# Weighing the values of two tiles together, with a third place for weights and the key norms one tile earlier

## The chip, the cores and the metric

The kernel runs on one core of a Trainium2 chip. The core has TensorE (PE in the profile), VectorE (DVE), ScalarE (ACT), GpSimd (POOL) and SyncE (SP), which issues the transfers here. Each engine works through its own queue of instructions and waits on semaphores that others raise. The metric is the time of one execution on the device in microseconds.

## The reference, cut to what matters

One perceiver layer for 128 queries of width 512, in fp32: a cross attention over 12544 rows of context, a self attention, and a mixture of experts. The change lies wholly in the cross attention, whose text part covers the 12287 context rows behind the first 257:

```python
q = rms_norm(linear(x, q_w, q_b), norm_q_w).reshape(B, L, NH, HD)
k = rms_norm(linear(ctx_txt, k_w, k_b), norm_k_w).reshape(B, -1, NH, HD)
v = linear(ctx_txt, v_w, v_b).reshape(B, -1, NH, HD)
img_x = attention(q, k_img, v_img)     # the 257 image rows, keys and values of their own
txt_x = attention(q, k, v)             # 16 heads of 32 channels, softmax over the rows
out = (txt_x + img_x).reshape(B, L, DIM)
```

## The kernel before

The text rows are cut into blocks of 512 rows (`blocks[1]` to `blocks[24]`; block 0 is the image part) and each block into four tiles of 128 rows, called j = 0 to 3 below. A tile has a running number t. Keys and values of a block come from seven quarter products each instead of eight (a Strassen scheme): `step(b, k)` computes product k of the keys (`kp`) and of the values (`vp`), and the sums of context quarters that it needs come from `ctx_sums` on POOL (L1058, tile `xs`).

For each tile, `scores` (L1159) multiplies keys by queries: 16 small matmuls on 32 rows of the array each, in tiling form 32*128, into the one PSUM tile `s`, which takes four of eight banks. `weights` (L1246) makes `p` from it: VectorE scales each row by `rinv` (the inverse norm of its key) and subtracts the bound `m_bc` (L1255), ScalarE takes the exponential (L1263). `weigh` (L1266) multiplies the values by `p` and adds to `avp`: 16 matmuls in form 128*32. `into_sums` (L1424, L1433) adds `p` to the running sums of weights `ls` on POOL. There are two places for `p` (pool `two`, tag `p`).

The norms of the keys go through four engines. When the keys of half a block are ready, `squares` (L1116) squares them on ScalarE, `add_squares` (L1123, rows L1127) folds the squares to one row of partitions' sums in two POOL instructions, `key_norms` (L1010, rows L1018 and L1029) sums over partitions with 16 tiny matmuls on PE in form 128*32 and scales on VectorE, and `inv_sqrt` (L815, row L818) raises to the power -1/2 on POOL, which gives `rinv`. Half 0 of a block serves its tiles 0 and 1, half 1 its tiles 2 and 3.

The main loop (L1535 to L1640) goes over the tiles of blocks 2 to 23. While it works on block b it makes the keys and values of block b+1. All instructions are pinned (`pin`), so each engine executes them in the order in which the program writes them. For a block b the order on the engines that matter is:

| tile | PE | POOL |
|---|---|---|
| j=0 | products 1; scores; weigh the tile before; products 2 | tile j=3 of the block before into the sums; `add_squares(b, 1)` |
| j=1 | products 6; scores; weigh; norms of b, half 1 | tile j=0 into the sums; `rinv` of b, half 1 |
| j=2 | products 5, 7 of keys; scores; weigh; products 3 | tile j=1 into the sums; in blocks 17 to 22 one scaling of later weights |
| j=3 | product 7 of values; scores; weigh; norms of b+1, half 0; products 4 | `add_squares(b+1, 0)`; tile j=2 into the sums; `ctx_sums(b+2)`; `rinv` of b+1, half 0 |

In the table `weigh` always means the tile before the one whose scores were just made (`weigh_pending`, L1448, with `pend`). The last block, 24, follows written out (L1642 to L1676), where the loads for the self attention begin (`early_loads`, L1486) as places come free. The place `mb`, which held the first bound, is free after tile 13; in block 15 two loads of weight codes go there (L1633 to L1635). Here t1 is the first text tile, `RENEWED` is 2, `SWITCH` is tile 13, `LAST` is 24, `AHEAD` is blocks 17 to 22.

Of the kernel before, what the change touches and what calls it, by code (L numbers as in the profile page):

```python
# [9 lines left out]
FP = mybir.dt.float32  # L10
# [5 lines left out]
P = 128  # L16
# [754 lines left out]
def fast_block(ctx: ExitStack, tc: tile.TileContext, a: dict, out: bass.AP, amiss: bass.AP):  # L771
# [78 lines left out]
    def load_codes(g, nm, t):  # L850

        codes[g, nm] = t.rearrange("p (c f) -> p c f", c=4)
        pin(nc.sync.dma_start(out=codes[g, nm], in_=a[f"w{nm}_codes"][g]))
# [28 lines left out]
    def slot(pool, tag, name):  # L882

        t = pool.tile([P, 2, 1024], FP, tag=tag, name=name)
        return [t[:, 0, :], t[:, 1, :]]
# [10 lines left out]
    with ExitStack() as xs:  # L896
# [226 lines left out]
        def add_squares(b, i):  # L1123

            ks = slice(i * HALF, (i + 1) * HALF)
            for w in (2, 1):
                pin(nc.gpsimd.tensor_tensor(  # L1127
                    sq[b][:, :w, ks], sq[b][:, :w, ks], sq[b][:, w : 2 * w, ks], op=ALU.add
                ))
# [318 lines left out]
        def weigh_pending():  # L1448
            k, pk = pend
            weigh(k, pk, k in (t1, SWITCH), k == SWITCH - 1)  # L1450
# [35 lines left out]
        def early_loads(j):  # L1486

            if j == 0:
                f = slot(two, "kraw", "f")
                homes[2].append(f[0])  # L1490
                load_codes(2, "v", f[0])
                homes[3] = [f[1]]
                load_codes(3, "q", f[1])
                homes["bv"] = slot(two, "ctx", "bv")
                wo.append(slot(xc, "kw", "wo_0"))
            elif j == 1:
                g = slot(two, "v", "g")
                homes[3] += g
                load_codes(3, "k", g[0])
                load_codes(3, "v", g[1])  # L1500
                t = row("kt", "sc_23", (P, 2, 3 * GW))
                load_scales(2, t[:, 0, :])
                load_scales(3, t[:, 1, :])
                for k, of in enumerate((a["bv"][:1024], a["bv"][1024:])):
                    pin(nc.sync.dma_start(out=homes["bv"][k], in_=of.partition_broadcast(P)))
                wo.append(slot(two, "ctx", "wo_1"))
                wo.append(slot(xc, "xsum", "wo_2"))
                pin(nc.sync.dma_start(
                    out=so, in_=a["wo_scales"].unsqueeze(1).to_broadcast([FEAT // BLOCK, 2, D])
                ))  # L1510
                load_wo(0)
            elif j == 2:
                h = slot(xc, "sq", "h")
                homes[4] = list(h)
                load_codes(4, "q", h[0])
                load_codes(4, "k", h[1])
                t = row("vt", "sc_45", (P, 2, 3 * GW))
                load_scales(4, t[:, 0, :])
                load_scales(5, t[:, 1, :])
                pin(nc.sync.dma_start(out=bo, in_=a["bo"].partition_broadcast(P)))  # L1520
                wo.append(slot(xc, "vw", "wo_3"))
                load_wo(1)
                load_wo(2)
# [3 lines left out]
        def load_wo(k):  # L1527
            for h in range(2):
# [2 lines left out]
                    out=wo[k][h].rearrange("p (j f) -> p j f", j=2), in_=a["wo_codes"][:, j : j + 2, :]  # L1531
                ))

        AHEAD = range(NB - 8, NB - 2)
        for t in range(tile0[2], tile0[LAST]):  # L1535
            b, part, o, m = tiles[t]
            j = t - tile0[b]


            make = step  # L1540
            if t == SWITCH + 3:
                pin(nc.tensor.matmul(
                    avp["txt"].rearrange("p g q -> p (g q)"),
                    lhsT=ident,
                    rhs=kept["av"],
                    start=False,
                    stop=False,
                    skip_group_check=True,
                ))
            late = make if b + 1 < LAST else (lambda *of: None)  # L1550
            if j == 0:
                make(b + 1, 1)
            elif j == 1:
                make(b + 1, 6)
            elif j == 2:
                make(b + 1, 5)
                late(b + 1, 7, "k")
            else:
                late(b + 1, 7, "v")
            if j == 3:  # L1560
                add_squares(b + 1, 0)
            if t == tile0[LAST] - 1:
                unsummed = pend
            else:
                into_sums(*pend)
            if j == 0:
                add_squares(b, 1)
            elif j == 2 and b in AHEAD:
                scale_weights((b - AHEAD[0]) // 3, "qkv"[(b - AHEAD[0]) % 3], nc.gpsimd)
            elif j == 3 and b + 2 < NB:  # L1570
                ctx_sums(b + 2)
            if t == SWITCH:
                m_bc["txt"] = m_new
            p, s = weights(t)
            weigh_pending()
            if j == 1:
                key_norms(b, [2, 3])
            elif j == 3 and b + 1 < LAST:
                key_norms(b + 1, [0, 1])
            pend = (t, p)  # L1580
            if t == tile0[RENEWED + 1]:
                m_new = xc.tile([P, 4, CHUNK], FP, tag="mx", name="mb_new")
                on_all(q_new, m_new, "new")
                pin(nc.vector.tensor_tensor(over, q_new, q_old, ALU.subtract))
                less = small.tile([P, XH], FP, tag="less", name="less")
                pin(nc.scalar.activation(less, over, AF.Exp, scale=-1.0))
            elif t == tile0[RENEWED + 1] + 1:

                shrink = rowp.tile([P, D], FP, tag="h", name="shrink")
                on_heads(less, shrink, "less")  # L1590
            elif t == SWITCH:
                av_old = avp["txt"].rearrange("p g q -> p (g q)")
                kept = {"av": row("kept_av", "kept_av")}
                pin(nc.vector.tensor_tensor(kept["av"], av_old, shrink, ALU.mult))
                avp["txt"] = ps_o.tile([P, NC, P], FP, tag="o", name="av_new")
            elif t == SWITCH + 2:
                lp = bank("l_old")
                for i in range(4):
                    r = slice(i * XHD, (i + 1) * XHD)
                    pin(nc.tensor.matmul(  # L1600
                        lp[r, :], lhsT=ones[:, :XHD], rhs=ls_old[i // 2][:, i % 2, :],
                        start=True, stop=True, skip_group_check=True,
                    ))
                kept["l"] = row("kept_l", "kept_l")
                pin(nc.vector.tensor_tensor(kept["l"], lp, shrink, ALU.mult))
            if j == 2:
                make(b + 1, 3, "k")
            if b <= RENEWED:
                largest(t, s)
            if j == 0:  # L1610
                make(b + 1, 2)
            elif j == 2:
                make(b + 1, 3, "v")
            elif j == 3:
                late(b + 1, 4)
                if b + 3 < NB:
                    load_ctx(b + 3)
            if t == tile0[RENEWED + 1] - 1:
                q_new = query_max(mx, P, "t1")
            if b == RENEWED + 3 and j == 0:  # L1620
                pin(nc.vector.reciprocal(l_img, l_img))
            if b == RENEWED + 3 and j == 1:
                flat = att_img.rearrange("p g q -> p (g q)")
                pin(nc.vector.tensor_tensor(flat, flat, l_img, ALU.mult))
            if b == RENEWED + 3 and j == 2:
                pin(nc.gpsimd.tensor_tensor(
                    att_img, att_img, vbs.unsqueeze(2).to_broadcast([P, NC, P]), op=ALU.add
                ))
            if b == AHEAD[0] - 2 and j == 0:
                for t_, nm in ((bq, "bq"), (bk, "bk"), (gw, "gate_w")):  # L1630
                    pin(nc.sync.dma_start(out=t_, in_=a[nm]))
                pin(nc.sync.dma_start(out=gb, in_=a["gate_bias"].partition_broadcast(P)))
                homes[2] = slot(xc, "mb", "q")  # L1633
                load_codes(2, "q", homes[2][0])
                load_codes(2, "k", homes[2][1])  # L1635
            if b == AHEAD[0] - 1 and j == 0:
                for g in range(2):
                    for nm, t in zip("qkv", homes[g]):
                        load_codes(g, nm, t)
                    load_scales(g, aw.tile([P, 3 * GW], FP, tag="sc", name=f"sc_{g}"))  # L1640
# [8 lines left out]
        key_norms(b, [0, 1])  # L1649
        ps = [weights(t, p=xc.tile([P, 4, CHUNK], FP, tag="vw", name="p_last"))[0]]  # L1650
        half_into_sums(unsummed[1], 1)
        weigh(k, p, False, False)
        half_into_sums(p, 0)
        step(b, 4, "k")
        add_squares(b, 1)
# [874 lines left out]
```

## Time and profile before

| what | value |
|---|---|
| time, median of 3 runs | 1071.18 us (1070.46 to 1071.69) |
| time of the profiled execution | 1070.2 us |
| its span, first to last instruction | 1068.5 us |
| granted clock of TensorE | 0.998 of full |
| main loop, blocks 5 to 22 (210.8 to 817.2 us): PE busy | 606.44 of 606.44 us |
| the same stretch: POOL, VectorE, ScalarE busy | 525.88, 309.99, 214.30 us |
| block 23 and the last block (817.2 to 862.9): PE busy | 44.65 of 45.7 us |
| transfers in the main loop / from 949.6 to the end | 40 / 348 GB/s |

A row of the timeline or of the groups names the engine, the line of the program, the operation and its output and inputs; a number of microseconds in brackets is idle time of the engine just ahead of it, with the instruction that released it. PE's matmuls overlap, so the difference of two starts says more than a duration. A wait of an engine that is not on the path costs nothing by itself.

### The profile page before, as it was taken

To read this page: it belongs to the slowest core of one execution; us is meant where nothing else is said; L and a number is where in the kernel's file an instruction comes from. 1 tells how busy PE (TensorE), PEld (TensorE's weight loads), DVE (VectorE), ACT (ScalarE), POOL (GpSimd) and SP (SyncE) were. 2 spreads that over 40 slices of the span, in tenths; PEclk is the share of its full clock that TensorE was granted. 3 is DMA by queue.
4 is the path that set the end of the run, shared out by engine and by line. 5 is a ranking of instruction groups with operands and counts; after the bars stand their busy time and mean duration, and the time that the engine had idled before them with its cause. 6 is when DMAs were issued, how large, how long until landed. Compare 5 with 4: busy or idle time off the path is not lost.

```text
span 1068.5 us, 24782 instructions
## 1 busy us (share of the span) xinstructions
PE 1051.4 (98%) x11076; PEld 826.6 (77%) x11076; DVE 541.1 (51%) x671; ACT 355.8 (33%) x438; POOL 694.8 (65%) x378
## 2 busy tenths in 40 slices
PE   9999999999999999999999999999999989999997
PEld 6778888888888888888888888888888769754332
DVE  3667854574445544455444554455444668432211
ACT  2353333333333333332333333333333424403111
POOL 2256888688988888888988789988899810000000
PEclk9999999999999999999999999999999999999999
DMA  8221021101111011110122301110110399619996
GB/s 318 86 81 41 2 87 44 41 1 41 40 41 40 2 40 41 40 36 7 41 84 106 99 26 41 41 40 3 39 41 2 123 361 382 229 64 410 415 413 247
DMA packets 43251, 113.24 MB, mean 106 GB/s; under 512 B 6720, under 2 KB 12032, under 8 KB 42112
## 3 DMA queue, kind: packets, MB, share of 16 engines
q1 hardware_dynamic: 43136, 111.57, 28.4%
q8 instruction: 89, 1.46, 0.5%
q14 instruction: 26, 0.21, 0.1%
HBM read 111.26 MB, written 0.29 MB: 104 GB/s over the span
## 4 chain that ended last, share of the span: by engine, by line
PE 92%; DVE 3%; POOL 2%; ACT 1%; DMA 1%; issue 0%; SPq 0%; DVEq 0%; ACTq 0%; POOLq 0%
PE kp L1082 28%; PE vp L1082 26%; PE sb L1166 9%; PE av_new L1272 8%; PE up L2117 5%; PE acc L2104 2%; PE qp L1776 1%; PE kp L1776 1%; PE yp L1934 1%; PE svp L1797 1%; PE y L2158 1%; PE vp L1234 1%; PE av_old L1272 1%; DVE p L1255 1%; DMA x<-in_x 1%; POOL sq L1127 1%
## 5 line engine op out<-in xcount | busy, mean ns | idle before, releaser
L1433 POOL TENSOR_TENSOR ls<-ls,p 128x2048 f32<-128x2048 f32 x79 | 359.7, 4553 | 21.3 <-ACT p L1263 21.3
L1263 ACT ACTIVATE p<-p 128x2048 f32<-128x2048 f32 (+1 forms) x95 | 179.9, 1894 | 444.5 <-DVE p L1255 432.9
L1255 DVE SCALAR_TENSOR_TENSOR p<-sb,rinv,mb_new 128x2048 f32<-128x2048 f32 (+1 forms) x86 | 200.0, 2326 | 129.4 <-POOL rinv L818 95.2
L1127 POOL TENSOR_TENSOR sq<-sq 128x512 f32<-128x512 f32 x96 | 96.0, 1000 | 98.2 <-ACT sq L1121 94.4
L1166 PEld LDWEIGHTS sb<-qT_txt,kraw 32*128 32x128 f32 (+1 forms) x3040 | 93.4, 186 | 32.0 <-issue 31.0
L1166 PE MATMUL sb<-qT_txt,kraw 32*128 32x128 f32 (+1 forms) x3040 | 111.5, 283 | 0.0
L1082 PE MATMUL kp<-xs,w_k_w 128*128 128x256 f32 x384 | 95.4, 391 | 0.0
L1082 PE MATMUL kp<-ctx,w_k_w 128*128 128x256 f32 x384 | 93.2, 386 | 1.0 <-ACT kp L1139 1.0
L1272 PE MATMUL av_new<-p,v 128*32 128x128 f32 (+1 forms) x2720 | 92.2, 276 | 1.0 <-ACT p L1263 1.0
L1082 PE MATMUL vp<-vt,xs 128*128 128x256 f32 x384 | 92.5, 384 | 0.0
L1082 PE MATMUL kp<-xs,kt 128*128 128x256 f32 x384 | 91.2, 380 | 0.1
L1082 PE MATMUL vp<-w_v_w,ctx 128*128 128x256 f32 x384 | 90.9, 380 | 0.0
L1082 PE MATMUL vp<-w_v_w,xs 128*128 128x256 f32 x384 | 90.8, 379 | 0.0
L1082 PEld LDWEIGHTS kp<-ctx,w_k_w 128*128 128x128 f32 x384 | 70.7, 190 | 15.0 <-issue 5.1
L1082 PEld LDWEIGHTS vp<-vt,xs 128*128 128x128 f32 x384 | 71.1, 190 | 13.3 <-ACT kraw L1110 4.5
L1082 PEld LDWEIGHTS kp<-xs,kt 128*128 128x128 f32 x384 | 72.5, 190 | 11.3 <-issue 1.1
L1082 PEld LDWEIGHTS vp<-w_v_w,xs 128*128 128x128 f32 x384 | 72.8, 190 | 10.1
L1082 PEld LDWEIGHTS vp<-w_v_w,ctx 128*128 128x128 f32 x384 | 72.8, 190 | 10.0 <-issue 0.2
L1272 PEld LDWEIGHTS av_new<-p,v 128*32 128x32 f32 (+1 forms) x2720 | 69.5, 109 | 12.3 <-ACT p L1263 2.1
L1082 PEld LDWEIGHTS kp<-xs,w_k_w 128*128 128x128 f32 x384 | 69.2, 189 | 12.6 <-issue 4.8
L818 POOL TENSOR_TENSOR rs_x<-ve_x,neghalf 128x1 f32<-128x1 f32 x3 | 1.7, 551 | 94.5 <-DVE ve_x L826 94.5
L1121 ACT ACTIVATE sq<-kraw 128x1024 f32<-128x1024 f32 x48 | 50.0, 1041 | 10.3 <-DVE kraw L1112 10.3
(460 smaller groups left out, 1442.3 us busy)
## 6 DMA issues: line engine op xcount, KB each, us to landing
ctx<-in_ctxT SPq DMA_DIRECT2D x23, 1024.0 KB, 4.9
wo<-in_experts SPq DMA_DIRECT2D x18, 512.0 KB, 9.0
wo<-in_wo_codes SPq DMA_DIRECT2D x8, 512.0 KB, 6.3
wq<-in_experts SPq DMA_DIRECT2D x8, 512.0 KB, 9.8
wk<-in_experts SPq DMA_DIRECT2D x8, 512.0 KB, 9.4
wv<-in_experts SPq DMA_DIRECT2D x7, 512.0 KB, 10.0
q<-in_experts SPq DMA_DIRECT2D x7, 512.0 KB, 10.1
f<-in_experts SPq DMA_DIRECT2D x7, 512.0 KB, 10.1
```

Of the source, the lines that this page charges most:

```text
L1082: pin(nc.tensor.matmul(t[:, h, :], lhsT=lhs, rhs=rhs, start=(first and h == 0 and c == 0), stop=(h == 1 and c == 1), skip_group_check=True,))
L1121: pin(nc.scalar.activation(sq[b][:, :, ks], kraw[b][:, :, ks], AF.Square))
L1127: pin(nc.gpsimd.tensor_tensor(sq[b][:, :w, ks], sq[b][:, :w, ks], sq[b][:, w : 2 * w, ks], op=ALU.add))
L1166: pin(nc.tensor.matmul(s[:m, i, g * P : (g + 1) * P], lhsT=kraw[b][rows, g, o : o + m], rhs=qT[part][rows, g, :], start=True, stop=True,))
L1234: pin(nc.tensor.matmul(vp[:m, :], lhsT=ctx_sb[0][:, c, o : o + m], rhs=vw["img"][:, c, :], start=(c == 0), stop=(c == NC - 1),))
L1255: pin(nc.vector.scalar_tensor_tensor(p[:m, k : k + n], s[:m, k : k + n], rinv[:m, t : t + 1], m_bc[part][:m, k : k + n], ALU.mult, ALU.sub ...
L1263: pin(nc.scalar.activation(p[:m, k : k + n], p[:m, k : k + n], AF.Exp))
L1272: pin(nc.tensor.matmul(avp[part][i * XHD : (i + 1) * XHD, g, :], lhsT=vv[b][:m, t - tile0[b], hd * XHD : (hd + 1) * XHD], rhs=p[:m, i, g * ...
L1433: pin(nc.gpsimd.tensor_tensor(d, d, src, op=ALU.add))
L1776: pin(nc.tensor.matmul(pp[:, k, :], lhsT=w[:, c, k * SHD : (k + 1) * SHD], rhs=hT2[:, c, :], start=(c == 0), stop=(c == NC - 1),))
L2104: pin(nc.tensor.matmul(acc, lhsT=lhsT, rhs=rhs, start=(n_acc == 0), stop=last))
L2117: pin(nc.tensor.matmul(up[r : r + m, :], lhsT=lhsT, rhs=w13_of((kind != "all", i), c), start=(c == 0), stop=(c == NC - 1), skip_group_chec ...
```

## The change

From block 5 on (`PAIRED`), four things differ. The tiles are weighed two at a time: at j=0 the tiles j=2 and j=3 of the block before, at j=2 the tiles j=0 and j=1; `waiting` holds them. Every third tile's `p` goes to the place `mb`, so there are three places in turn. `key_norms` of a block's half 1 moves from j=1 to j=0, behind the pair of weighings. `add_squares` of half 1 moves on POOL ahead of the tile that is added at j=0. As `mb` is in use through the loop, the two loads of codes that stood in block 15 move to `early_loads(0)` in the last block, ahead of the load into `f`. In the last block all waiting tiles are weighed at the place where one was.

```diff
@@ early_loads
             if j == 0:
                 f = slot(two, "kraw", "f")
+                homes[2] = slot(xc, "mb", "q")
+                load_codes(2, "q", homes[2][0])
+                load_codes(2, "k", homes[2][1])
                 homes[2].append(f[0])
                 load_codes(2, "v", f[0])
@@ main loop
+        PAIRED = RENEWED + 3
+        waiting = [pend]
         AHEAD = range(NB - 8, NB - 2)
         for t in range(tile0[2], tile0[LAST]):
...
             if j == 3:
                 add_squares(b + 1, 0)
+            elif j == 0 and b >= PAIRED:
+                add_squares(b, 1)
             if t == tile0[LAST] - 1:
                 unsummed = pend
             else:
                 into_sums(*pend)
-            if j == 0:
+            if j == 0 and b < PAIRED:
                 add_squares(b, 1)
...
-            p, s = weights(t)
-            weigh_pending()
-            if j == 1:
+
+            p = None
+            if b >= PAIRED and (t - tile0[LAST]) % 3 == 0:
+                p = xc.tile([P, 4, CHUNK], FP, tag="mb", name=f"p_{t}")
+            p, s = weights(t, p=p)
+            if b < PAIRED or j % 2 == 0:
+                for k, pk in waiting:
+                    weigh(k, pk, k in (t1, SWITCH), k == SWITCH - 1)
+                waiting = []
+            waiting.append((t, p))
+            if j == (1 if b < PAIRED else 0):
                 key_norms(b, [2, 3])
             elif j == 3 and b + 1 < LAST:
                 key_norms(b + 1, [0, 1])
...
-                homes[2] = slot(xc, "mb", "q")
-                load_codes(2, "q", homes[2][0])
-                load_codes(2, "k", homes[2][1])
@@ last block
-        weigh(k, p, False, False)
+        for k_, p_ in waiting:
+            weigh(k_, p_, False, False)
```

## The prediction

> **What bounds the kernel now.** I read the page first: how long the span is, which engine fills it, and what the chain that ended last consists of.
>
> ```profile
> span 1068.5 us, 24782 instructions
> PE 1051.4 (98%) x11076; PEld 826.6 (77%) x11076; DVE 541.1 (51%) x671; ACT 355.8 (33%) x438; POOL 694.8 (65%) x378
> PE 92%; DVE 3%; POOL 2%; ACT 1%; DMA 1%; issue 0%; SPq 0%; DVEq 0%; ACTq 0%; POOLq 0%
> ```
>
> TensorE (PE) is the bound. Next, the waits: who stood still for whom in total, how many times, and the longest.
>
> ```profile
> DVE p L1255 <- POOL rinv L818: 95.2, 20, 5.0
> POOL sq L1127 <- ACT sq L1121: 94.4, 25, 19.2
> ```
>
> Once in each of 20 blocks VectorE waits nearly 5 us for a `rinv` that comes out of POOL. That is free today, since PE does not wait for it, but it says that at one place POOL runs late. The timeline of PE over one block (four tiles; scores are L1166, weighing L1272, key norms L1018, products L1082) shows what a tile costs between products:
>
> ```profile
> 412.85 1.17 PE L1166 MATMUL sb<-qT_txt,kraw 32*128 32x128 f32 x32
> 413.95 1.08 PE L1272 MATMUL av_new<-p,v 128*32 128x128 f32 x32
> 414.96 1.99 PE L1082 MATMUL kp<-ctx,w_k_w 128*128 128x256 f32 x8
> ...
> 422.15 1.17 PE L1166 MATMUL sb<-qT_txt,kraw 32*128 32x128 f32 x32
> 423.25 1.08 PE L1272 MATMUL av_new<-p,v 128*32 128x128 f32 x32
> 424.15 0.28 PE L1018 MATMUL ssq<-ones,sq 128*32 128x1 f32 x16
> 424.36 1.99 PE L1082 MATMUL kp<-xs,w_k_w 128*128 128x256 f32 x8
> ...
> 431.85 1.99 PE L1082 MATMUL kp<-xs,w_k_w 128*128 128x256 f32 x8
> ```
>
> Columns are start and duration; matmuls overlap, so I take differences of starts. The next fence is the same view of POOL around the same block: the sums of squares of the first half, a tile into the running sums, four context sums, the two `rinv`, a tile, and only then the squares of the second half.
>
> ```profile
> 402.70 2.07 POOL L1127 TENSOR_TENSOR sq<-sq 128x512 f32<-128x512 f32 x2 [3.95 <-ACT sq L1121]
> 404.74 4.57 POOL L1433 TENSOR_TENSOR ls<-ls,p 128x2048 f32<-128x2048 f32 x1
> 409.25 1.29 POOL L1064 TENSOR_TENSOR xs<-ctx 128x512 f32<-128x512 f32 x1
> ...
> 414.41 0.70 POOL L818 TENSOR_TENSOR rinv<-ms,neghalf 128x2 f32<-128x2 f32 x1
> 415.08 4.56 POOL L1433 TENSOR_TENSOR ls<-ls,p 128x2048 f32<-128x2048 f32 x1
> 419.58 2.09 POOL L1127 TENSOR_TENSOR sq<-sq 128x512 f32<-128x512 f32 x2
> 421.63 4.55 POOL L1433 TENSOR_TENSOR ls<-ls,p 128x2048 f32<-128x2048 f32 x1
> ```
>
> The squares of the second half end at 421.63, and the norms of them start on PE at 424.15: in time, with 2.5 us to spare. That margin is what the change spends.
>
> **The change, part by part.** Blocks 5 to 23 (19 of them) are touched. I call the four tiles of a block j = 0 to 3 and the products by kind and number (3k is product 3 of the keys).
>
> *PE's own work.* Prices, all differences of starts: scores to weighing 1.10; weighing to norms 0.90; weighing to a product 1.01; norms to a product 0.21. Scores straight to a full-array matmul happens at 852.76 (to 853.86): 1.10; with 85-column weights at 34.83 it was 1.05. Scores straight to norms happens once, at 52.95: 1.11, then 0.23 to the product. A second weighing behind the first I price at 0.90, the nearest row of the same array shape; 1.01 is its upper end. Tile by tile, before to after: j=0, 2.11 to 1.10+0.90+0.90+0.21 = 3.11 (+1.00); j=1, 2.21 to 1.10 (-1.11); j=2, 2.11 to 1.10+0.90+1.01 = 3.01 (+0.90); j=3, 2.21 to 1.34 (-0.87). Sum -0.08 a block, -1.5 us over 19. Weighing in pairs saves little because the norms at j=3 stay alone behind their scores.
> The Trainium skill ("TensorEngine Tiling (Array Packing)", Key Properties) says that a change of tiling mode drains the array, and "TensorE: Matmul & The Clock Gate" (Single matmul latency) puts a drain at about 175 ns. A block would go from 12 changes to 11; by the pages, an estimate, that is 19 x 0.175 = 3.3 us saved, against 1.5 by the rows.
>
> *The norms of the second half, from j=1 to j=0.* On PE they now stand right behind the pair of weighings, ahead of products 2 and 6; everything queued behind them waits with them. They need the squares' sums of the second half, which on POOL now stand before the tile at j=0, but still behind the tile of j=3, the context sums and `rinv`. I count both engines from the start of 3k (431.85).
> PE to the norms: 3k, 3v, 7v 5.38 (to the scores at 437.23); scores and norms of j=3 1.11+0.23; 4k, 4v, 1k, 1v 7.10 (405.75 to 412.85); scores 1.10; two weighings 1.80. PE arrives at 16.72.
> POOL to the end of the second half: 3k's last VectorE step ends at 434.76, 2.91 after 3k; ScalarE squares it 1.04 with hand-overs of 0.03 and 0.07, so POOL begins at 4.05 (ScalarE is free: the exponential of j=2 ends 2.6 after 3k, as 3k comes one weighing later). First half 2.04 (402.70 to 404.74), tile 4.51, context sums 5.16 (409.25 to 414.41), `rinv` 0.67, second half 2.05 (419.58 to 421.63): 18.48. With 0.06 to release PE (an exponential ended at 843.77, its weighing began at 843.83), PE goes on at 18.54. **PE stands still for 1.82 us in every block.** No cover exists: PE is the bound and takes its work in order.
> From there to the next 3k: norms 0.21, products 2 and 6 7.19 (414.96 to 422.15), scores 1.10, 5k, 5v, 7k 5.38 (424.36 to 429.74), scores 1.10, weighings 0.90+1.01: 16.89. Period 18.54+16.89 = 35.43, against 33.70 before (the products 3k in the chain start 33.7 apart). It is a closed loop, PE to VectorE to ScalarE to POOL to PE, so nothing catches up later: +1.73 a block.
> The skill speaks against this placing too: "TensorE: Matmul & The Clock Gate" (Part 3, The mechanism) says matmuls start and end strictly in order, so products behind waiting norms cannot pass; the trace agrees, product 4k behind a weighing held to 843.83 began only at 844.84.
>
> *First and last block.* In block 5 only one tile waits to be weighed; the second half ends at 415.08+2.05 = 417.13, so PE goes on 4.34 after the scores at 412.85, and 3k comes 16.89 later, at 21.23 instead of 19.00: +2.23. Blocks 6 to 23 add 18 x 1.73 = 31.1. After 3k of block 23 the path leaves PE: squares, POOL, `rinv`, the weights of the last block. There 3k comes 0.90 later after its scores, and squares 0.40 later (7.06 after the scores instead of 839.06-832.40 = 6.66); the scores of j=3 then wait less than half a microsecond for VectorE, and I put 0.1 to 0.2 more on the last `rinv`. So +33.3 at 3k, -0.90+0.55 behind it: about +33.
>
> *A third place for weights.* `p` of a tile now overwrites that of three tiles earlier, weighed at the latest one j=0 or j=2 before and summed by POOL two tiles before. No row shows VectorE waiting for a place today: its waits at L1255 are put down to `rinv`, to scores, and for 0.5 us at j=3 to POOL's squares, which end (438.43) as the scores begun at 437.23 do. Gain zero; if the cover were gone a wait would lie under PE's 1.82.
>
> *Loads.* Two loads of 512 KB leave block 15 and go ahead of `f` on SP's queue in the last block: two issues of 0.3 to 0.4. Their place comes free when POOL has summed tile 92 (836.83), before `f`'s (issue at 839.44 after the scores of tile 94), so SP stands no longer. They land in 5 to 6 us; the first reader scales them at 880.8. Zero; if the loads behind them were on the path, 1 MB at the 415 GB/s of the late slices is 2.5 us.
>
> *Small moves.* VectorE's step for the norms sits behind the weights of j=0, which end at 18.85, the norms at 18.8: no wait. POOL's second `rinv` comes behind a tile, at 23, needed at 33. Zero.
>
> Sum: +33 us. The profiled execution has 1070.2 us (span 1068.5 and 1.7 around it), so 1103.2; the median, 1071.2, lies 1.0 above it: 1104.2.
>
> **Rivals.**
> *The sums are in time.* If POOL's second half ended 1.82 us earlier, PE would not stop; time 1071.2-1.5+0.5 = about 1070, not slower. Against: `rinv`, the step just before, is seen to release VectorE at 415.15 in 20 blocks. This decides from a POOL lead of 1.8 us.
> *A smaller wait.* If POOL kept its distance to the scores of j=0 instead of 3k, it would end at 417.19 against 415.75 on PE: 1.44 less the 0.08, 1.36 x 18 + 2.2 = 27 us: 1098. Half of that, if hand-overs hide some: 1085.
> *A longer loop.* A hand-over of 0.45, as the issue time before ScalarE's squares at 837.49 in the chain, added once a block: 8 us more, 1112.
> *The loads bind.* 2.5 us on top: 1107. Against: 40 us until they are read.
>
> **How the numbers follow.** Forecast with its near variants (1095 to 1112) 0.82; a smaller wait below 1095 0.07; longer than 1112 0.04; in time, or no change that shows, 0.07, of which 0.05 is faster by over 0.2% (scores to a product at 1.05 and nothing lost in the last block: 1071.2 - 19 x 0.13 = 1068.7) and 0.02 within 0.2%, about what a measurement of this kernel can tell from no change. So slower 0.93. Range 1095 to 1112: the smaller wait at its full 27 us with a little less, and the longer loop.
>
> **What would show it.** Right: a wait of PE's norms (or their weight load) on POOL's squares L1127, 1.8 us in some 19 places, 34 us; blocks 35.4 apart; PE's share falling to about 95%; two weighings together taking 1.80 to 1.91; VectorE still idle before `rinv`. Wrong: norms starting straight behind the weighings with a block of 33.6; PE waiting at `p` or at products instead; a lower granted clock from the new gaps; loads in the last block late.

## The result and the profile after

The changed kernel takes 1130.67 us in the median of 5 runs (1129.66 to 1132.30), against 1071.69 us of the kernel before on the same chip: a ratio of 1.0553, 95% interval 1.0542 to 1.0564. It is slower by 59 us. The direction was forecast, the size was not: 1104 us and a range up to 1112 were on record. The profiled execution of it has a span of 1128.8 us. From its page, the span, TensorE's line and the chain that ended last:

```profile
span 1128.8 us, 24820 instructions
PE 1077.6 (95%) x11076; PEld 845.6 (75%) x11076; DVE 539.3 (48%) x671; ACT 362.3 (32%) x438; POOL 694.2 (61%) x378
PE 66%; POOL 24%; DVE 4%; ACT 3%; issue 1%; DMA 0%; SPq 0%; ACTq 0%; POOLq 0%; DVEq 0%
```

POOL has come into the chain with 24% of the span, where it had 2%. The second thing to see is in PE's line: it is busy for 26.2 us longer than before (1077.6 against 1051.4) with the same 11076 matmuls. Waiting does not make an engine busier, so some matmuls themselves have become slower. The waits (total, times, longest) show the new one on PE beside VectorE's old one:

```profile
DVE p L1255 <- POOL rinv L818: 103.5, 20, 5.6
...
PE ssq L1018 <- POOL sq L1127: 34.3, 19, 2.2
```

PE's norms wait for POOL's squares once in each of the 19 blocks. One block in the timeline of PE, from the scores of j=0 to those of j=1 (start, duration, idle time before it in brackets):

```profile
430.08 1.17 PE L1166 MATMUL sb<-qT_txt,kraw 32*128 32x128 f32 x32
431.18 1.95 PE L1272 MATMUL av_new<-p,v 128*32 128x128 f32 x64
434.93 0.31 PE L1018 MATMUL ssq<-ones,sq 128*32 128x1 f32 x16 [1.79 <-POOL sq L1127]
435.17 1.99 PE L1082 MATMUL kp<-ctx,w_k_w 128*128 128x256 f32 x8
...
442.27 1.17 PE L1166 MATMUL sb<-qT_txt,kraw 32*128 32x128 f32 x32
```

And POOL in the same block: context sums and the inverse root still stand ahead of the squares of half 1, which end at 434.87, and 0.06 us later PE goes on.

```profile
426.95 1.29 POOL L1064 TENSOR_TENSOR xs<-ctx 128x512 f32<-128x512 f32 x1
...
432.13 0.70 POOL L818 TENSOR_TENSOR rinv<-ms,neghalf 128x2 f32<-128x2 f32 x1
432.79 2.08 POOL L1127 TENSOR_TENSOR sq<-sq 128x512 f32<-128x512 f32 x2
```

The forecast had a wait of 1.82 us and a block of 35.43; here they are 1.79 and 35.48 (norms of j=3 at 422.74, then at 458.22). But this is one of the quick blocks. In 14 of the 19, the same stretch looks like this:

```profile
323.49 0.31 PE L1018 MATMUL ssq<-ones,sq 128*32 128x1 f32 x16 [1.79 <-POOL sq L1127]
323.72 3.27 PE L1082 MATMUL kp<-ctx,w_k_w 128*128 128x256 f32 x8
...
332.51 1.17 PE L1166 MATMUL sb<-qT_txt,kraw 32*128 32x128 f32 x32
```

The wait is the same, yet from the norms to the scores of j=1 it takes 9.02 us instead of 7.34. Nobody holds PE up: the eight matmuls behind the wait take 3.27 us in place of 1.99. The view by stretches says why (stretch, its length, then busy time and instructions of PE, its weight loads, VectorE, ScalarE, POOL; the third number from the end is the granted clock):

```profile
321.50:324.28 2.78, 0.99 (x27) 0.73 (x20) 2.43 (x2) 0.47 (x1) 2.70 (x3) 1.00 0.00 0
324.28:327.70 3.42, 3.42 (x10) 2.70 (x9) 0.00 (x0) 2.11 (x3) 3.42 (x1) 0.50 0.02 5
327.70:330.00 2.30, 2.30 (x12) 2.04 (x11) 0.00 (x0) 0.76 (x2) 2.30 (x3) 1.00 0.00 0
```

TensorE's clock was granted at half for 3.42 us, beginning 0.8 us after PE had gone on. In the mean of the 14 blocks the stretch takes 9.03 us, so half a clock costs 9.03 - 7.34 = 1.69 us each time. So the 57.3 us by which the scores of tile 93 (j=2 of block 23) come later (832.40 before, 889.70 after) split into 14 x 1.69 = 23.6 us of clock and 33.7 us of all else, the waits less what the pairs save, for which 32.4 had been forecast. The last block adds 0.8 us up to the first reciprocal (862.93 and 921.05; forecast 0.55), one more half-clock stretch at the output projection 1.2 us, and the stages after it 1.0 us, which I have not followed up.

### The profile page after: what moved, and what is told of

It is laid out like the page before. It is cut to its first block, busy times and chain, and to the rows that moved or that the text cites. A ratio compares the mean times of both kernels' runs of the same rounds, so it can differ in the third digit from the quotient of the medians.

```text
span 1128.8 us, 24820 instructions
## 1 busy us (share of the span) xinstructions
PE 1077.6 (95%) x11076; PEld 845.6 (75%) x11076; DVE 539.3 (48%) x671; ACT 362.3 (32%) x438; POOL 694.2 (61%) x378
## 4 chain that ended last, share of the span: by engine, by line
PE 66%; POOL 24%; DVE 4%; ACT 3%; issue 1%; DMA 0%; SPq 0%; ACTq 0%; POOLq 0%; DVEq 0%
PE kp L1082 21%; PE vp L1082 14%; POOL ls L1433 8%; POOL sq L1127 7%; PE sb L1166 6%; PE up L2130 4%; PE av_new L1272 3%; PE acc L2117 2%; POOL xs L1065 2%; POOL xs L1066 2%; POOL xs L1064 2%; POOL xs L1067 2%; ACT sq L1121 2%; POOL rinv L818 1%; DVE kraw L1112 1%
## 5 line engine op out<-in xcount | busy, mean ns | idle before, releaser
L1082 PE MATMUL kp<-ctx,w_k_w 128*128 128x256 f32 x384 | 109.2, 435 | 1.0 <-ACT kp L1139 1.0
L1082 PE MATMUL vp<-w_v_w,ctx 128*128 128x256 f32 x384 | 99.2, 405 | 0.0
L1082 PEld LDWEIGHTS vp<-w_v_w,ctx 128*128 128x128 f32 x384 | 80.9, 211 | 14.0 <-issue 0.2
L1082 PEld LDWEIGHTS kp<-ctx,w_k_w 128*128 128x128 f32 x384 | 79.1, 211 | 14.7 <-ACT kp L1139 1.4
L1272 PE MATMUL av_new<-p,v 128*32 128x128 f32 (+1 forms) x2720 | 84.6, 274 | 0.5 <-ACT p L1263 0.5
L1144 DVE TENSOR_TENSOR kz<-kp,kp 128x512 f32<-128x512 f32 x24 | 16.6, 691 | 129.9 <-PE kp L1082 122.3
L1272 PEld LDWEIGHTS av_new<-p,v 128*32 128x32 f32 (+1 forms) x2720 | 71.8, 110 | 7.1 <-ACT p L1263 1.4
```

What stands on the lines that cost most here:

```text
L1082: pin(nc.tensor.matmul(t[:, h, :], lhsT=lhs, rhs=rhs, start=(first and h == 0 and c == 0), stop=(h == 1 and c == 1), skip_group_check=True,))
L1272: pin(nc.tensor.matmul(avp[part][i * XHD : (i + 1) * XHD, g, :], lhsT=vv[b][:m, t - tile0[b], hd * XHD : (hd + 1) * XHD], rhs=p[:m, i, g * ...
```

## The experiments

The theory to be tested: the whole loss comes from the norms of half 1 standing at j=0, where they wait for POOL, and from the clock that this wait lowers. The rivals: pairs, third place or loads cost something by themselves; the slow products have another reason than the clock; the wait has another than POOL's order.

**Norms back to j=1, all else as changed.**

```diff
-            if j == (1 if b < PAIRED else 0):
+            if j == 1:
                 key_norms(b, [2, 3])
```

> The norms of half 1 go back to j=1; pairs, the third place, POOL's order and the moved loads stay. Theory (the whole loss comes from the norms standing at j=0, where PE waits 1.79 us for POOL, and from the clock that the wait drops): PE no longer waits for POOL's squares, the granted clock is 0.998, a block costs 2.99+1.34+2.99+1.34 = 8.66 between its products against 8.64 before, so 1071 to 1073 us. Rival (weighing in pairs, the third place or the moved loads cost time of their own): well above 1073; if they were the whole cause, 1130.

Measured: 1070.39 us against 1071.16 before, ratio 0.9994 (0.9984 to 1.0003), clock 0.998. The wait is gone from PE's list, and blocks are 33.62 apart (33.70 before). So one line of the change carries the whole loss, and the pairs, the place and the loads carry none. It also shows that pairs gain next to nothing when the norms stand alone at two tiles: the 0.08 us of a block are not theirs but product 6 of the values, which in the kernel before took 1.90 us up to the next scores (420.25 to 422.15) and here takes 1.82.

**Norms alone at j=0, on the kernel before.**

```diff
+            elif j == 0 and b >= PAIRED:
+                add_squares(b, 1)
...
-            if j == 1:
+            if j == (1 if b < PAIRED else 0):
                 key_norms(b, [2, 3])
```

> The kernel before with one part of the change alone: the norms of half 1 at j=0 and their squares first on POOL at j=0; no pairs, no third place, loads where they were. Theory: only one weighing stands ahead of the norms, so PE arrives 0.9 us earlier and waits about 2.3 us; POOL's squares start 4.54 after product 3 of the keys, as before, so a block takes 19.03+17.00 = 36.03 (+2.33), 19 of them +44 us, and the longer wait drops the clock in 13 blocks or more, +22 to +32: 1137 to 1147 us. Rival (the pairs cause the loss): 1071 us. Rival (the norms cause the wait, but the clock drops come from the pairs): 1115 us.

Measured: 1144.39 us, ratio 1.0686 (1.0668 to 1.0704), slower than the whole change. The timeline of PE in one block:

```profile
437.37 1.08 PE L1272 MATMUL av_new<-p,v 128*32 128x128 f32 x32
440.57 0.40 PE L1018 MATMUL ssq<-ones,sq 128*32 128x1 f32 x16 [2.13 <-POOL sq L1127]
440.90 3.50 PE L1082 MATMUL kp<-ctx,w_k_w 128*128 128x256 f32 x8
```

The wait is 2.13 us (40.6 in 19 places), and the clock is at half for 3.41 us in all 19 blocks, which are 37.55 us apart. That is where the regularity of it shows: 37.55 is 11 times 3.413. Within an execution of either kernel all half-clock stretches begin on one grid of 3.41 us (in the changed kernel at 286.74, 324.28, 361.83, 399.38, 471.06 and so on: distances of 11, 11, 11 and 21 steps), and a block that has just the length of 11 steps meets the grid at the same point each time. Here the loop moves to that point: in the first block the half clock begins 0.14 us after PE has gone on, and from the fourth block on within 0.03 us of it. Where it begins late, norms to scores take 8.97 us, where it begins with PE, 8.93; that this is what holds the loop in step with the grid is likely, but no run tests it.

**The wait filled with idle matmuls.**

```diff
-        def key_norms(b, js):
+        def key_norms(b, js, fill=0):
...
             sp = bank(f"ssq_{b}_{js[0]}")
+            keep_warm(fill, sp[:, P:])
...
-                key_norms(b, [2, 3])
+                key_norms(b, [2, 3], fill=0 if b < PAIRED else 7)
```

> The changed kernel with seven idle matmuls of 128 columns (about 0.23 us each, 1.6 us) put ahead of the norms at j=0, where PE stands still for 1.79 us; their output is not read. Theory (the wait is 33 us, and 14 half-clock stretches of 3.41 us, each costing 1.69, are 24 us more): blocks stay 35.5 apart, since POOL still sets the end, but no clock drop is left in the loop: 1131 - 24 = 1107 us, mean clock 0.99 or more. Rival (products after the wait are slow for another reason, such as work that bunches up on the other engines): slow blocks of 37.2 stay, 1130 us. Second rival (the filling delays PE): above 1131.

Measured: 1105.63 us, ratio 1.0327 (1.0310 to 1.0344), clock 0.998. The timeline of PE:

```profile
424.56 1.96 PE L1273 MATMUL av_new<-p,v 128*32 128x128 f32 x64
426.45 1.83 PE L845 MATMUL ssq<-ones 128*128 128x128 f32 x14
428.29 0.31 PE L1019 MATMUL ssq<-ones,sq 128*32 128x1 f32 x16
...
435.63 1.17 PE L1167 MATMUL sb<-qT_txt,kraw 32*128 32x128 f32 x32
```

The idle matmuls (x14 is the seven of them, each with two records, as the 16 of a weighing have 32) take up the wait, the norms start no earlier than POOL lets them (blocks are 35.46 apart), but now every block goes from the norms to the next scores in 7.34 us, and no stretch of the loop is at half clock. 25 us have come back by giving PE useless work. With that the two parts are shown apart: 1105.6 - 1071.2 = 34.4 us that stay at full clock (the forecast's +33), and about 25 us of clock (the traces have 23.6 in the loop and 1.2 at the output projection).

**A shorter wait.**

```diff
-                pin(inv_sqrt(rinv[:m, t0 + j0 : t0 + j1], ms[:m, j0:j1]))
+                if later:
+                    put_off.append((rinv[:m, t0 + j0 : t0 + j1], ms[:m, j0:j1]))
+                else:
+                    pin(inv_sqrt(rinv[:m, t0 + j0 : t0 + j1], ms[:m, j0:j1]))
...
             elif j == 0 and b >= PAIRED:
                 add_squares(b, 1)
+                while put_off:
+                    pin(inv_sqrt(*put_off.pop(0)))
...
-                key_norms(b + 1, [0, 1])
+                key_norms(b + 1, [0, 1], later=b + 1 >= PAIRED)
```

> The changed kernel with POOL's inverse root of half 0 (0.67 us) moved from before to behind the squares of half 1. Theory: PE's wait shrinks from 1.79 to 1.12 us, so a block without a clock drop takes 35.47-0.67 = 34.80; a wait of 1.12 is well under half of a 3.41 us window and drops no clock. From the changed kernel, 1131 - 19 x 0.67 - 24 = 1094 us. Rival (any wait of over a microsecond drops the clock): 34.80 + 1.69 in most blocks, 1115 to 1120 us. Rival (the wait is not set by POOL's order): 1131.

Measured: 1098.16 us, ratio 1.0250 (1.0233 to 1.0268). The row of PE's waits:

```profile
PE ssq L1020 <- POOL sq L1132: 21.4, 19, 1.5
```

1.1 us a block as reckoned (the first block has the 1.5), and no half clock in the loop. The 4 us above the forecast are in the block: 35.09 us instead of 34.80, because the weights of j=0, behind a later inverse root, delay ScalarE's copies, and products 6 then wait for a bank (1.92 us each where 1.73 to 1.82 is usual).

**One idle matmul instead of seven.**

```diff
-                key_norms(b, [2, 3], fill=0 if b < PAIRED else 7)
+                key_norms(b, [2, 3], fill=0 if b < PAIRED else 1)
```

> The changed kernel with one idle matmul (instead of seven) ahead of the norms at j=0: PE's wait of 1.79 us shrinks to about 1.4 without moving the end of it. Theory (the clock drops when more than half of a 3.41 us window, 1.7 us, is idle): no drop in the loop, blocks of 35.5, 1105 to 1107 us as with seven. Rival (a wait of 1.4 us still drops it): 14 drops or so, up to 1131.

Measured: 1107.23 us in two runs, ratio 1.0333 (1.0314 to 1.0351). The wait is 1.33 to 1.36 us in the usual block and there is no half clock, with one exception, in a block in which it was 1.56 us:

```profile
782.51 0.31 PE L1019 MATMUL ssq<-ones,sq 128*32 128x1 f32 x16 [1.56 <-POOL sq L1128]
782.75 2.63 PE L1083 MATMUL kp<-ctx,w_k_w 128*128 128x256 f32 x8
```

So the forecast of the time holds; the limit of half a window, 1.7 us, that the expectation had, holds nearly, but not exactly. In the changed kernel all 14 drops come 0.40 to 1.62 us after PE went on, so that all of the wait lay inside one step of the grid, the 3.41 us before the drop. In four of the five blocks without a drop a line of the grid cuts the wait, and 1.42 to 1.70 us of it lie inside one step; the first block had 1.83 there and no drop. The same can be counted in the profiled executions of all ten kernels of this document, from 10 us on to the last work, with PE's idle time added up in each step of the grid: of 34 steps with 1.75 us or more, 33 were followed by half clock; of six with 1.67 to 1.70 us, three; of all with less, one, the 1.56 here. Matmuls' ends are modelled, and the wait by the profile is not the time in which the array stood still, so nothing sharper follows from these runs.

**Third place and loads alone.**

```diff
-            elif j == 0 and b >= PAIRED:
-                add_squares(b, 1)
...
-            if j == 0 and b < PAIRED:
+            if j == 0:
                 add_squares(b, 1)
...
-            if b < PAIRED or j % 2 == 0:
+            if True:
                 for k, pk in waiting:
...
-            if j == (1 if b < PAIRED else 0):
+            if j == 1:
                 key_norms(b, [2, 3])
```

> The kernel before with only the third place for weights and the two loads moved to the last block; each tile is weighed by itself, norms and squares stand where they were. Theory (both are free): 1071 us, ratio 0.998 to 1.002, granted clock as before. Rival (1 MB more among the loads of the last block holds up the self attention): +2.5 us, 1073.7.

Measured: 1071.29 us against 1071.44, ratio 1.0003 (0.9992 to 1.0013). Both are free, within this tenth of a per cent.

**Squares of half 1 ahead of the context sums.** The first experiment removed the wait by giving up the place of the norms; this one keeps their place and gets POOL ready instead.

```diff
-            elif j == 0 and b >= PAIRED:
-                add_squares(b, 1)
...
-            elif j == 3 and b + 2 < NB:
+            elif j == 3 and b + 2 < NB and b + 1 < PAIRED:
                 ctx_sums(b + 2)
...
                 late(b + 1, 4)
+                if PAIRED <= b + 1 < LAST:
+                    add_squares(b + 1, 1)
+                    ctx_sums(b + 2)
```

> The whole change, but POOL's order at j=3 is: tile j=2 into the sums, inverse root of half 0, squares of half 1, and only then the context sums. Theory: the squares of half 1 are ready some 13.3 us after product 3 of the keys, PE reaches their norms at 16.7, so nothing waits and the clock stays; a block costs PE 3.13+1.10+2.99+1.34 = 8.56 between its products, against 8.64 before, and loses the small stall before product 6 of the values (0.08): 33.5 against 33.70, 19 of them -3.6, last block +0.8: 1068 us, ratio 0.997. Rival (the context sums, now 2.7 us later, hold up product 6): PE waits at that product and the time is 1071 or more. Rival (norms at j=0 cost something beyond POOL's order): 1080 or more.

Measured: 1067.82 us against 1071.44, ratio 0.9965 (0.9952 to 0.9979): the whole change with POOL's order mended is 0.35% faster than the kernel before. The timeline of PE:

```profile
411.97 1.95 PE L1272 MATMUL av_new<-p,v 128*32 128x128 f32 x64
413.74 0.28 PE L1018 MATMUL ssq<-ones,sq 128*32 128x1 f32 x16
413.95 2.00 PE L1082 MATMUL kp<-ctx,w_k_w 128*128 128x256 f32 x8
```

The norms follow the pair at once. A block is 33.48 us.

**Two visits a block.** If the gain of pairs is that the array changes its form less often, it should grow when the weighing stands only where norms stand. The edit comes on top of the one before.

```diff
-            if b >= PAIRED and (t - tile0[LAST]) % 3 == 0:
-                p = xc.tile([P, 4, CHUNK], FP, tag="mb", name=f"p_{t}")
-            p, s = weights(t, p=p)
-            if b < PAIRED or j % 2 == 0:
+            s = scores(t, "b") if b >= PAIRED else None
+            if b < PAIRED:
+                p, s = weights(t, p=p)
+            if b < PAIRED or j in (0, 3):
                 for k, pk in waiting:
                     weigh(k, pk, k in (t1, SWITCH), k == SWITCH - 1)
                 waiting = []
+            if b >= PAIRED:
+                if (t - tile0[LAST]) % 3 == 0:
+                    p = xc.tile([P, 4, CHUNK], FP, tag="mb", name=f"p_{t}")
+                p, s = weights(t, s=s, p=p)
```

> As the kernel with the squares before the context sums, but the tiles are weighed at j=0 (one: j=3 of the block before) and at j=3 (three: j=0 to 2), each time next to the norms that stand there anyway, so that the array changes its form for weighing and norms twice a block. Theory (what pairs gain is only the changes of form): 2.21+1.10+1.10+4.01 = 8.42 a block against 8.64, and the small stall of 0.08: 33.4, 19 x -0.30 = -5.7 us, 1065 to 1067 us, ratio 0.995. The weights of j=3 wait for their place until tile j=0 is weighed, about 1 us after the scores, with 7 us until the next scores. Rival (that later start, or three weighings ahead of product 4, delays squares and POOL): PE waits show up, 1071 or more.

Measured: 1064.79 us against 1071.44, ratio 0.9941 (0.9927 to 0.9955), the fastest of all. The timeline of PE at j=3, three weighings in one go:

```profile
435.21 2.83 PE L1272 MATMUL av_new<-p,v 128*32 128x128 f32 x96
437.86 0.28 PE L1018 MATMUL ssq<-ones,sq 128*32 128x1 f32 x16
```

A block is 33.34 us. Counting the changes of the array's form in a block: 12 with the norms back at j=1 (33.62 us), 11 with the squares ahead (33.48), 10 here (33.34): 0.14 us for one change. The three kernels do the same work in a block, and none has a wait of PE in it.

## Why the prediction was right or wrong

- *PE's own work, -0.08 a block.* Right in kind, and somewhat too small: where nothing waits (squares ahead of the context sums), a block is 0.22 us shorter than before. Of that 0.14 is the pairs' one change of form less, for which 0.08 had been reckoned, and 0.08 is product 6 of the values, which was not in the sum. The row prices held: a pair and the product behind it took 1.88 us (1.91 reckoned), a pair up to its norms 1.77 (1.80), scores to a product 1.10. The Trainium skill puts a drain at about 175 ns ("TensorE: Matmul & The Clock Gate", Single matmul latency); the runs show 0.14 us for a change of form.
- *The norms at j=0 and the closed loop, 1.82 us of waiting and +1.73 a block.* Right to 0.05 us: 1.79, and 35.44 to 35.48 a block where the clock stayed. The kernel with the wait filled, which holds just this part, came out at 1105.6 us, against the forecast of 1104.
- *"From there to the next 3k", 16.89 us, in it "products 2 and 6 7.19".* This is the step that failed. It took the products behind the wait from rows of the kernel before, at full clock, and so priced the wait as idle time and nothing more; what the wait does to the clock of the work behind it was left at zero, without a reason. In 14 of 19 blocks these products took 8.79 us: the clock was at half for 3.41 of them, which costs 1.69 us a block, 23.6 us in the loop, and there was one more such stretch at the output projection (1.2 us). The text named "a lower granted clock from the new gaps" among the signs of being wrong, but put neither a price nor a chance on it, and gave 0.04 to a time above 1112. The kernel before had stops of PE of 1.40 us (58.01 to 59.41 us) and 1.47 us at a full clock, but after its start none as long as 1.8, so its trace gave no ground for the zero. An upper end with a half clock behind every wait, 19 x 1.7 = 32 us more, would have held the result.
- *First and last block.* Right within 0.3 us each: in block 5 the product 3k came 21.18 us after the scores of j=0 (21.23 reckoned), and the last block added 0.8 (0.55 reckoned). The 18 blocks between added 31.9 us in the kernel with the wait filled (31.1 reckoned).
- *Third place, loads, small moves at zero.* Right for place and loads, 1.0003 alone; the small moves were not tried by themselves.
- *Rivals.* "In time" did not happen by itself, but the kernel with the squares first is just that case, and better than its 1070. The "longer loop" had the right sign and the wrong cause.

## What to carry to other kernels

A wait of TensorE where it bounds the kernel can have two prices: its own length, and what the clock does to the dense matmuls behind it; look at the granted clock in the stretch behind the wait, not at the mean of the run, which had only fallen from 0.998 to 0.976. Before moving a consumer earlier, walk the producer's queue to what stands ahead of it: here the squares were moved ahead of one POOL instruction, a tile's sum, while six others (a tile, four context sums, an inverse root) still stood ahead of them, and the order of those was a better cure than the consumer's old place (ratios 0.9965 and 0.9994 to the kernel before). And grouping small matmuls of one array form gains by the changes of form that it removes, so what else has that form belongs into the group.

## What the runs showed of the hardware that I had not expected

- The clock of TensorE fell to half after waits of 1.8 us (14 of 19) and 2.1 us (19 of 19), held there for 3.41 us each time, and every such stretch began on a grid of 3.413 us that runs through the whole execution. What tells these cases apart best is how much of the wait lay in one step of the grid: 33 of the 34 steps with 1.75 us or more of idle time were followed by half clock. A loop whose block has the length of 11 steps of this grid met it in every block.
- The Trainium skill ("TensorE: Matmul & The Clock Gate", Part 1) gives the window as 3413 ns and free-running, which these rows confirm. It gives an idle window of about 3.4 us as what throttles; here a stop of about half of that was enough.
- Seven matmuls a block whose output nobody reads made the changed kernel 25 us faster (1105.6 against 1130.7).
- All ten kernels have a stop of 1.47 us ahead of the output projection (L1691 before). The clock fell behind it in the profiled executions of the changed kernel, of the shorter wait and of the third place alone, and stayed in the other seven. The step of the grid had 1.68 us of idle time in those three, and 1.16 to 1.68 in the others, depending on where the stop met the grid. It costs 1.2 to 1.3 us, so differences of that size between two executions of such a kernel say nothing by themselves.
